# Ten input loads of a transformer block go to ScalarE's DMA queue, the others ahead of the row copies on SyncE's

## The chip, the cores and the metric

One NeuronCore of a Trainium2 chip runs the whole program. The metric is the device time of one execution in microseconds (us); the compared value is the median of several runs. A separate execution was taken with the hardware profiler; all tables and views come from that one.

## What is computed

A float32 block over x of 8 x 512 x 256: layer norm, 16-head attention, layer norm, residual, then a feed-forward layer with a top-1 choice among 8 low-rank experts, layer norm, residual. Cut to what matters:

```python
x_proj = (x @ w_in.T + b_in).reshape(b, l, h, -1)      # after layernorm of x
q, k, v = jnp.split(x_proj, 3, axis=-1)
att = softmax(jnp.einsum('blhd,bmhd->blmh', q, k) * scale, axis=2)
opt = jnp.einsum('blmh,blhd->blhd', att, v).reshape(b, l, d)
x = x + _layernorm(opt @ w_out.T + b_out)
...
top1 = argmax(softmax(x @ gate_W.T + gate_b))
base = x @ wi_W.T + wi_b
for i in range(8):
    inter = relu(base + (x @ lora_A[i].T) @ lora_B[i].T)
    out = out + (top1 == i) * (inter @ wo_W.T + wo_b)
x = x + _layernorm(out)
```

In the einsum for opt the key index m appears in att alone, so att is summed over it. The kernel forms all scores, their row maxima, exponentials and sums, as the reference does.

## The kernel before

The eight sequences are worked on one after another; a sequence has 512 tokens, in four chunks of 128 rows, and its 16 heads are taken in eight pairs. Every float32 operand of a matmul is split into a high and a low part (names that end in h and l), and a product is made of three matmuls. TensorE's projections (`psqk`, `psv`), the scores (`sc`), the output projection (`psy`) and the feed-forward layer (`psh`, `psz`) all run this way, the scores with the split laid out in rows by DMA.

The work is recorded as operations with an engine, a cost and a due time; a planner (`Plan.order`) plays them through and writes one list, and `settle` then moves some of them by hand. The program is emitted in the order of that list, so each engine gets its own part of the list in that order, and executes it strictly in order.

The head of the program, in the order in which its steps depend on each other:

- `load_x` (line 263) loads a sequence into `xt_b`; the first comes in two halves of 256 KB, the others in one piece of 512 KB. `load` (line 276) loads a weight; `fetch` (line 314) cuts a large weight into loads of 256 KB: `wv`, `wout`, and `wi_0` to `wi_3`, `wo_0` to `wo_3`. All of them are issued by SyncE.
- `first_weights` (line 1098): ScalarE scales `wqk_0` and makes its high part `wqkh`, VectorE its low part `wqkl`; then the same for `wqk_1`. These are ScalarE's first operations.
- `prepare` (line 496) for sequence 0: VectorE's statistics `st_x`, `mv_x` and the normalized `ln_x`; transposes `pst_xn` on TensorE; ScalarE's high part `xnh`, VectorE's low part `xnl`. On VectorE `wqkl` of `wqk_0` stands ahead of `ln_x`.
- `project` (line 536): six matmuls for each of four `psqk` tiles; ScalarE's and VectorE's parts go to `hl`.
- `lay_out_q` and `lay_out_k` (lines 579 and 559): SyncE copies `hl` to `q` and `rows`, two copies for each pair of heads, so that a score product has high and low parts in one pass.
- `scores` (line 618): the product `sc` on TensorE, the maximum `nmax` on VectorE, the exponential on ScalarE.
- `gate_weights` (line 1144): VectorE's `lbh` and `lbs` from `lb`; `wga` from `wga_f`. GpSimd splits `wv`, `wout`, `wi` and `wo`; before them it has the small operation `calm` (line 1250), which reads `ln_x`.

`warm_up` (line 1064) issues 30 matmuls on constants at the start.

In the built program every DMA signals one of eight completion semaphores, which are given out in turn. A DMA is issued only when the one that used its semaphore before has landed; the issuing engine waits for it, and so does what stands behind it on that engine. Before the change SyncE's order is: xt_0 (two), wqk_0, wqk_1, bqk, wv, wout, lb, wi_0 to wi_3, xt_1, xt_2, xt_3, wga_f, gb, low, bv, bout, wob, q_0 (two), rows_0 (two), q_1, rows_1, wo_0 to wo_3, q_2, rows_2, rows_3 and so on. The ninth, wi_0, is the first with a wait of this kind, for xt_0's first half; wga_f waits for lb, q_0 for xt_2 and xt_3.

In the part of `settle` at the change, `behind(last, ops)` takes `ops` out of the list and puts them in right after `last`; `of(engine, names...)` finds operations by the tile they write; `turns` are VectorE's first three operations that write `hl` of sequence 0.

Of the kernel before, what the change touches and what calls it, by code (L numbers as in the profile page):

```python
# [26 lines left out]
PE, ACT, DVE, POOL, DMA = "PE", "ACT", "DVE", "POOL", "DMA"  # L27
# [155 lines left out]
def kernel(  # L183
# [18 lines left out]
    nc = tc.nc  # L202
# [45 lines left out]
    def const_tile(shape, dtype, name, parts=1):  # L248
        return plan.tile(const, shape, dtype, name, 1, name)
# [6 lines left out]
    behind = [0.0]  # L256

    def landing(size):

        behind[0] = max(0.0, behind[0] + size / DMA_RATE - DMA_COST)  # L260
        return DMA_DELAY + size / DMA_RATE + behind[0]

    def load_x(b):
        t = xts[b] = plan.tile(io, [P, NC, D], F32, "xt", XB, f"xt_{b}")
        m = X0 if b == 0 else NC
        for c in range(0, NC, m):
            plan.op(
                DMA, DMA_COST,
                lambda c=c: nc.sync.dma_start(
                    out=t()[:, c : c + m],  # L270
                    in_=x[b].rearrange("(p c) d -> p c d", c=NC)[:, c : c + m],
                ),
                writes=[t], lag=landing(m * P * D * 4),
            )

    def load(name, src, shape=None, rows=P, place=None):

        shape = shape or list(src.shape)
        if place is None:
            t = const_tile(shape, F32, name)  # L280
        else:
            t = plan.tile(place[0], shape, F32, *place[1:], name)
        plan.op(
            DMA, DMA_COST, lambda: nc.sync.dma_start(out=t()[:rows], in_=src), writes=[t],
            lag=landing(rows * np.prod(src.shape[1:]) * 4),
        )
        return t

    def on_all_partitions(name, src):
        return load(name, src.partition_broadcast(P), [P, src.shape[0]])  # L290
# [23 lines left out]
    def fetch(name, src, *places):  # L314

        fs = flat(src).rearrange("p (c d) -> p c d", d=D)
        return [
            load(f"{name}_{i}", fs[:, 2 * i : 2 * i + 2], [P, 2, D], place=places[i % len(places)])
            for i in range(fs.shape[1] // 2)
        ]  # L320
# [23 lines left out]
    for i in range(2):  # L344
        t = const_tile([P, 2 * P], F32R, f"axs{i}")
# [146 lines left out]
    def units(b):  # L492

        return (0, 1), (2, 3)
# [590 lines left out]
    def fetch_first():  # L1085
        parts = [
            load(f"wqk_{dc}", wqk[:, dc], [P, 2, NG, P], place=(work, "full", FB))
            for dc in range(ND)
        ]
        return load("bqk", bqk), parts  # L1090

    during(-9000, "first", load_x, 0)
    wqk_in = during(-8990, "first", fetch_first)
    during(5000, "warm", warm_up)
# [36 lines left out]
    for g in range(NG):  # L1131
        during(-7000 if g == 0 else 0, f"project0{g}", project, 0, g)
        for p in range(NP * g, NP * (g + 1)):
            during(-6000 + 2 * p, "k0", lay_out_k, 0, p)
    during(0, "x1", load_x, 1)
    wv_h, wv_l = during(0, "wv", weight, "wv", wv.shape, wv_in, (POOL, POOL))

# [46 lines left out]
    for b in range(B):  # L1184
        t = 2 * STEPS * b
        if b + 2 < B:
            behind[0] = 0.0
            during(t, "load", load_x, b + 2)

        apart = units(b) if b in APART else [(0, 1, 2, 3)]  # L1190
        for i, cs in enumerate(apart):
            for p in range(NPR):
                at = t + STEPS * i + p * len(cs)
                during(at if b or i else at - 6000, "q" if b or i else "q0", lay_out_q, b, p, cs)
                scores(b, cs, p, at)
        if b + 1 < B:
            during(t, "prepare", prepare, b + 1)
            for g in range(NG):
                during(t, f"project{g}", project, b + 1, g)
                for p in range(NP * g, NP * (g + 1)):  # L1200
                    n = 2 if b + 1 in APART else 4
                    during(t + n * p, "k", lay_out_k, b + 1, p)
        for u in range(len(units(b))):
            tu = t + STEPS * (u if b in APART else 1)
            left = 2 * B - 1 - (2 * b + u)
            k = f"_{left}" if left < 3 else f"_first{u}" if b == 0 else f"{u}"
            during(tu, "v" + (k if b == 0 else ""), values, b, u)
            during(tu, "attend" + k, attend, b, u)
            during(tu, "feed" + k, feed, b, u)

    def settle(done):


        def of(eng, *marks):
            return [o for mark in marks for o in done if o.eng == eng and o.mark == mark]

        def behind(last, ops):
            for o in ops:
                done.remove(o)
            i = done.index(last) + 1  # L1220
            done[i:i] = ops


        behind(of(DVE, "ln_x_0_2")[-1], of(DVE, "bqk"))
        lbh = of(DVE, "lbh_0", "lbh_512")
        behind(of(DVE, "xnl_0")[-1], lbh)
        st2, turns = of(DVE, "st_x_2"), of(DVE, "hl_0_0_0", "hl_0_0_1", "hl_0_1_0")
        st1, maxes = of(DVE, "st_x_1"), of(DVE, "nmax_0_0_1_1", "nmax_0_2_0_1")
        behind(turns[0], st1[:2])
        behind(turns[1], st1[2:] + of(DVE, "mv_x_1"))  # L1230
        behind(turns[2], st2[:2])
        behind(maxes[0], st2[2:] + of(DVE, "mv_x_2"))
        behind(of(DVE, "nmax_0_2_0_1")[0], of(DVE, "st_x_3", "mv_x_3"))
        lbs = of(DVE, "lbs")
        behind(of(DVE, "nmax_0_1_1_1")[0], lbs[:1])
        behind(of(DVE, "nmax_0_3_0_1")[0], lbs[1:])
        behind(of(DVE, "nmax_0_4_1_1")[0], of(DVE, "wga"))


        nr = [[o for o in done if o.eng == POOL and o.mark == f"nr_x_{i}"] for i in range(4)]  # L1240
        wih, wil = of(POOL, "wih"), of(POOL, "wil")
        woh, wol = of(POOL, "woh"), of(POOL, "wol")
        behind(of(DVE, "mv_x_1")[-1], nr[1] + [wih[2], wil[2], wih[3], wil[3]])
        behind(of(DVE, "mv_x_2")[-1], nr[2])
        behind(of(POOL, "ln_x_2_2")[-1], nr[3])
        behind(
            [o for o in of(POOL, "ln_x_3_0")][-1], [woh[0], wol[0], woh[1], wol[1]]
        )
        behind(of(POOL, "hl_1_0_0")[-1], [woh[2], wol[2], woh[3], wol[3]])
        calm = Op()  # L1250
        calm.eng, calm.mark = POOL, None
        calm.fn = lambda: nc.gpsimd.tensor_scalar(
            calm_sb(), state[0]["xn"]()[:, 1, :1], 1.0, 0.0, ALU.mult, ALU.add
        )
        last = of(DVE, "ln_x_0_2")[-1]
        early = [o for o in done[done.index(nr[0][-1]) + 1 : done.index(last)] if o.eng == POOL]
        behind(last, early)
        done.insert(done.index(last) + 1, calm)


        rows = []
        for p in range(NP):
            if p < X1B:
                rows += of(DMA, f"q_0_{p}")
            rows += of(DMA, f"rows_0_{p}")
            if p == 1:
                rows += of(DMA, "wo_0", "wo_1", "wo_2", "wo_3")
        behind(turns[1], rows)


        extra = of(PE, "psu")[FIRST:]
        return [o for o in done if o not in extra]

    done = settle(plan.order())

    name = f"{B - 1}_{units(B - 1)[-1][0]}"
# [70 lines left out]
DMA_COST = 440.0  # L1347
# [20 lines left out]
XB = 4  # L1368
# [72 lines left out]
```

## Time and profile before

| | |
|---|---|
| median of 3 runs | 516.54 us (516.49 to 519.35) |
| profiled execution, time | 513.44 us |
| profiled execution, span from the first to the last instruction | 511.6 us |
| mean granted TensorE clock | 0.963 of full speed |
| busy: TensorE / VectorE / ScalarE / GpSimd | 95% / 91% / 85% / 76% of the span |
| chain that ended last | PE 62%, DVE 24%, ACT 4%, DMA 3% |
| loads, KB and us from issue to landing | xt_0 halves 256 KB 2.7; wqk 256 KB 4.4 and 4.6; wv 4.3; wout 4.7; wi 256 KB 6.4; wo 256 KB 4.5 (median); xt_1 to xt_3 512 KB 7.8 (median); rows 128 KB 2.9 (median) |

PE is TensorE, DVE VectorE, ACT ScalarE, POOL GpSimd, SP SyncE; SPq is SyncE's work of issuing DMAs. Times are counted from the span's start. The span lies 1.8 us under the time of its own execution, and that time 3.1 us under the median of the timed runs. The table shows averages; the head of the program has its own limits, which have to be read from the timeline and the chain of waits there.

### The profile page before, as it was taken

The page shows a single profiled execution, that of the slowest core. Times are in us where ns is not written, and L with a number is a line of the kernel's source. Part 1 is how long each engine was busy: PE and PEld are TensorE (multiplying, and loading weights), DVE is VectorE, ACT ScalarE, POOL GpSimd, SP SyncE. Part 2 cuts the span into 40 slices and gives each one's busy share as a digit, 9 for nine tenths or more (in the row PEclk, how much of TensorE's full clock was granted, in tenths as well). Part 3 has the DMA queues.
Part 4 walks back from the last instruction along what each step waited for, and adds up shares of the span by engine and source line. Part 5 has one row for each costly group of instructions (what it writes and reads, how often), then busy time and mean ns, then how long its engine had stood idle before and what let it go on. Part 6 is the DMA issues. An engine that isn't in the chain of part 4 may idle for free.

```text
span 511.6 us, 11203 instructions
## 1 busy us (share of the span) xinstructions
PE 483.8 (95%) x3134; PEld 423.7 (83%) x3134; DVE 467.3 (91%) x1056; ACT 436.4 (85%) x1205; POOL 390.1 (76%) x615
## 2 busy tenths in 40 slices
PE   7769989999999999999999999999999999998995
PEld 6534837879888988989989988989899988998995
DVE  6788999999999999999999999999999999998633
ACT  3569999998999999998999899999999989995210
POOL 7867455565889987997979998696878767888652
PEclk9955879999999999999999999999999999999999
DMA  8772263334423443244423442244224432200001
GB/s 273 217 196 68 52 154 71 89 69 112 111 51 106 113 111 68 69 121 104 105 50 120 101 102 75 51 113 110 66 70 94 114 87 67 48 26 2 21 22 42
DMA packets 41182, 46.56 MB, mean 91 GB/s; under 512 B 11326, under 2 KB 28222, under 8 KB 41120
## 3 DMA queue, kind: packets, MB, share of 16 engines
q1 hardware_dynamic: 41120, 45.84, 35.2%
q8 instruction: 26, 0.43, 0.3%
q14 instruction: 36, 0.29, 0.2%
HBM read 8.05 MB, written 4.19 MB: 24 GB/s over the span
## 4 chain that ended last, share of the span: by engine, by line
PE 62%; DVE 24%; ACT 4%; DMA 3%; issue 2%; SPq 2%; POOL 1%; POOLq 0%; ACTq 0%; DVEq 0%
PE sc L642 16%; PE psz L486 14%; DVE nmax L661 13%; PE psh L486 12%; PE psqk L486 7%; PE psy L486 3%; ACT sc L670 3%; PE psv L486 3%; PE psh L960 2%; DVE st_x L399 2%; PE sc L651 1%; DMA q<-hl 1%; DMA rows<-hl 1%; DVE hTh L300 1%; PE pst_x L469 1%
## 5 line engine op out<-in xcount | busy, mean ns | idle before, releaser
L670 ACT ACTIVATE sc<-sc,nmax 128x512 f32<-128x512 f32 x512 | 342.6, 689 | 17.1 <-DVE nmax L661 10.6
L661 DVE TENSOR_REDUCE nmax<-sc 128x1 f32<-128x512 f32 x512 | 325.4, 678 | 9.2 <-PE sc L651 4.2
L642 PE MATMUL sc<-rows,q 128*128 128x512 f32 x480 | 182.6, 423 | 5.6 <-ACT sc L670 3.1
L670 ACT ACTIVATION_READ_ACCUMULATOR sc<-sc,nmax 128x1 f32 x512 | 120.6, 236 | 0.0
L642 PEld LDWEIGHTS sc<-rows,q 128*128 128x128 f32 x480 | 88.7, 192 | 25.7 <-ACT sc L670 18.7
L486 PE MATMUL psz<-woh,hTh 128*128 128x256 f32 x256 | 73.0, 285 | 0.8 <-DVE xnl L528 0.5
L486 PE MATMUL psh<-x2h,wih 128*128 128x256 f32 x256 | 73.0, 285 | 0.0
L486 PE MATMUL psz<-woh,hTl 128*128 128x256 f32 x256 | 72.2, 282 | 0.0
L486 PE MATMUL psz<-wol,hTh 128*128 128x256 f32 x256 | 72.1, 282 | 0.0
L486 PE MATMUL psh<-x2h,wil 128*128 128x256 f32 x256 | 72.0, 281 | 0.0
L486 PE MATMUL psh<-x2l,wih 128*128 128x256 f32 x256 | 72.0, 281 | 0.0
L306 POOL TENSOR_TENSOR hTl<-full_h,hTh 128x512 fp32r<-128x512 f32 x44 | 56.9, 1294 | 2.3 <-DVE hTh L300 1.1
L486 PEld LDWEIGHTS psz<-wol,hTh 128*128 128x128 f32 x256 | 48.2, 188 | 3.6
L486 PEld LDWEIGHTS psh<-x2l,wih 128*128 128x128 f32 x256 | 48.2, 188 | 3.2
L486 PEld LDWEIGHTS psz<-woh,hTh 128*128 128x128 f32 x256 | 48.2, 188 | 2.1 <-POOL hTl L306 0.7
L486 PEld LDWEIGHTS psh<-x2h,wih 128*128 128x128 f32 x256 | 48.3, 189 | 1.1 <-DVE y L777 0.2
L486 PEld LDWEIGHTS psz<-woh,hTl 128*128 128x128 f32 x256 | 48.2, 188 | 0.2 <-POOL hTl L306 0.2
L486 PEld LDWEIGHTS psh<-x2h,wil 128*128 128x128 f32 x256 | 48.2, 188 | 0.0
L306 POOL TENSOR_TENSOR hl<-full_qk,hl 128x512 fp32r<-128x512 f32 x28 | 36.3, 1295 | 1.2
L384 ACT ACTIVATE full_h<-psh 128x512 f32<-128x512 f32 x44 | 26.4, 605 | 8.6 <-PE psh L960 8.1
L298 POOL TENSOR_SCALAR hl<-full_qk 128x512 fp32r<-128x512 f32 x28 | 17.3, 619 | 18.2 <-ACT full_qk L384 17.5
L486 PE MATMUL psqk<-xnh,wqkh 128*128 128x512 f32 x64 | 27.6, 431 | 0.7 <-ACT xnh L521 0.7
(132 smaller groups left out, 1021.4 us busy)
## 6 DMA issues: line engine op xcount, KB each, us to landing
rows<-hl SPq DMA_DIRECT2D x128, 128.0 KB, 2.6
q<-hl SPq DMA_DIRECT2D x480, 32.0 KB, 2.0
out<-ln_z SPq DMA_DIRECT2D x15, 256.0 KB, 2.2
xt<-in_x SPq DMA_DIRECT2D x7, 512.0 KB, 3.8
wi<-in_wi SPq DMA_DIRECT2D x4, 256.0 KB, 6.4
q<-hl SPq DMA_DIRECT2D x16, 64.0 KB, 2.2
wo<-in_wo SPq DMA_DIRECT2D x4, 256.0 KB, 4.5
xt<-in_x SPq DMA_DIRECT2D x2, 256.0 KB, 2.7
```

The costliest lines, as they stand in the source:

```text
L298: nc.gpsimd.tensor_scalar(pick_hi(), pick(), 1.0, 0.0, ALU.mult, ALU.add)
L300: nc.vector.tensor_copy(pick_hi(), pick())
L306: e.tensor_tensor(pick_lo(), pick(), f32(pick_hi()), ALU.subtract)
L384: lambda: nc.scalar.activation(full(), flat(ps()), func, **kw()),
L399: DVE, 335, lambda c=c: nc.vector.bn_stats(st()[:, c, :], sel()[:, c, :]),
L469: nc.tensor.transpose(ps()[:, dc, c * P : (c + 1) * P], src()[:, c, dc * P : (dc + 1) * P], ident(),)
L486: nc.tensor.matmul(ps, w, xx, start=start and i == 0, stop=stop and i == len(terms) - 1)
L642: nc.tensor.matmul(sc(), q()[:, e, cols], k(), start=True, stop=True)
L651: nc.tensor.matmul(sc(), q()[rows, 0, cols], k()[rows], start=True, stop=True)
L661: lambda sc=sc, nmax=nmax: nc.vector.tensor_reduce(nmax(), sc(), AX.X, ALU.max, negate=True),
L670: lambda sc=sc, nmax=nmax, esum=esum, i=i, h=h: nc.scalar.activation(sc(), sc(), AF.Exp, bias=nmax(), accum_out=esum()[:, i, h : h + 1]),
L960: nc.tensor.matmul(ps()[:, i, :], lbs()[:KL, fs], axs()[:KL, : n * P], start=False, stop=i == 1,)
```

## The change

```diff
@@ load_x
-                lambda c=c: nc.sync.dma_start(
+                lambda c=c: (nc.scalar if 0 < b < XB else nc.sync).dma_start(
@@ load
+        queue = nc.scalar if name.split("_")[0] in ("wv", "wout", "lb", "wi") else nc.sync
...
-            DMA, DMA_COST, lambda: nc.sync.dma_start(out=t()[:rows], in_=src), writes=[t],
+            DMA, DMA_COST, lambda: queue.dma_start(out=t()[:rows], in_=src), writes=[t],
@@ settle
+        behind(
+            of(DMA, "bqk")[-1],
+            of(
+                DMA, "wv_0", "wout_0", "lb", "xt_1", "wi_0", "wi_1", "wi_2", "wi_3", "xt_2", "xt_3",
+                "bv", "low", "wo_0", "wo_1", "wo_2", "wo_3", "wga_f", "gb", "bout", "wob",
+            ),
+        )
+
         rows = []
         for p in range(NP):
             if p < X1B:
                 rows += of(DMA, f"q_0_{p}")
             rows += of(DMA, f"rows_0_{p}")
-            if p == 1:
-                rows += of(DMA, "wo_0", "wo_1", "wo_2", "wo_3")
         behind(turns[1], rows)
```

XB is 4, so xt_1, xt_2 and xt_3 go to ScalarE's queue. The orders of TensorE, VectorE and GpSimd are those of before; ScalarE's differs by the ten loads, and SyncE's by the loads. The built program has them in these orders, with the load whose landing each one waits for in brackets:

- ScalarE: wv, wout, lb, xt_1, wi_0 [xt_0, second half], wi_1 [lb], wi_2 [wqk_0], wi_3 [xt_1], xt_2 [bv], xt_3 [wi_1]; then the load of the activation table, and the first operation on wqk_0.
- SyncE: xt_0 (two), wqk_0, wqk_1, bqk [wv], bv [xt_0, first half], low [wout], wo_0 [wqk_1], wo_1 [bqk], wo_2 [low], wo_3 [wi_0], wga_f [wi_2], gb [wo_0], bout [wi_3], wob [wo_1], q_0 [xt_2; wo_2], rows_0 [wo_3; xt_3], q_1, rows_1, q_2, rows_2, rows_3 and so on.

## The prediction

> **What bounds the kernel now.** I read the shares of the chain of waits first, for what sets the end, and then only the head in order of time, because the change touches nothing behind the first 25 us. TensorE is on 62% of that chain and VectorE on 24%; no transfer is waited for in the steady part. So whatever the head loses or wins is handed on whole to the end, unless a stage behind it has slack. The chain in order of time (start, length, what), cut to the head:
>
> ```profile
> 1.64 4.38 DMA wqk<-in_wqk
> ...
> 6.04 0.43 ACT wqk L1106
> ...
> 6.49 0.64 ACT wqkh L302
> ...
> 7.77 1.38 DVE ln_x L452 x4
> ...
> 11.02 2.97 DVE lbh L1166 x2
> ...
> 25.60 3.82 DMA rows<-hl
> ...
> 30.36 1.28 DVE nmax L661 x2
> ```
>
> The head is a string of short steps that begins when ScalarE gets wqk at 6.04. VectorE's ln_x stands in VectorE's order behind wqkl_0, which waits for ScalarE's wqkh_0; the transposes wait for ln_x, the projections for the transposes. From 18 to 25.6 the chain runs along SyncE, which issues rows one after another; then VectorE's maxima take over. Second, the timeline of the issuing engine and of ScalarE's first instruction (start, length, engine, line, what):
>
> ```profile
> 0.72 1.28 ACT L1106 ACT_TABLE_LOAD   x1 [0.72 <-PEq L1425]
> 0.73 0.87 SPq L269 DMA_DIRECT2D xt<-in_x  x2
> 4.52 2.56 SPq L284 DMA_DIRECT2D wi<-in_wi  x4
> 7.13 2.02 SPq L269 DMA_DIRECT2D xt<-in_x  x3
> 10.71 0.33 SPq L284 DMA_DIRECT2D wga_f<-in_wga  x1
> 21.67 2.01 SPq L284 DMA_DIRECT2D wo<-in_wo  x4
> ```
>
> ScalarE's table load is free today: it lies in the 5.3 us before wqk lands. SyncE is through with xt_3 at 9.15 and then stands until 10.71. Third, the queue's own waits up to 40 us (who waited for what: total, times, longest):
>
> ```profile
> SPq L593 <- DMA xt<-in_x: 1.6, 2, 0.9
> SPq L284 <- DMA lb<-in_lb: 1.5, 1, 1.5
> ```
>
> That is the fact on which all turns: a load waits for the landing of the load that last used its completion semaphore, and everything queued behind it on the issuing engine waits too. wga_f stood 1.5 us for lb; q_0 stood for xt_2 and xt_3. Fourth, the head cut into stretches of TensorE's clock window (TensorE, its weight load, VectorE, ScalarE, GpSimd busy; granted clock; DMA):
>
> ```profile
> 17.06:20.48 3.42, 2.73 (x18) 2.14 (x16) 1.14 (x3) 0.65 (x2) 3.17 (x6) 1.00 0.49 118
> 20.48:23.89 3.41, 0.74 (x4) 0.30 (x4) 3.00 (x5) 3.01 (x10) 2.67 (x3) 0.88 0.67 166
> 23.89:27.30 3.41, 1.38 (x4) 0.79 (x4) 3.41 (x11) 2.89 (x9) 2.06 (x5) 0.50 0.90 301
> ```
>
> One window with 0.74 us of work, and the clock is halved.
>
> **The ten loads on ScalarE.** They stand in front of everything ScalarE computes, the table load included, and six of them wait: wi_0 for xt_0's second half, wi_1 for lb, wi_2 for wqk_0, wi_3 for xt_1, xt_2 for bv, xt_3 for wi_1. Issuing alone: wv 0.43, wout 0.43, lb 0.47, five and more at the same lengths (wi 4 x 0.43 at most, xt 3 x 0.64), some 0.05 between: 5.4 us, so ScalarE could be free at 6.1 and, after the table load of 1.28, at 7.4. That is 1.4 later than now and the floor.
>
> The waits ask for more. The chain is lb lands, wi_1 is issued, wi_1 lands, xt_3 is issued. I count kilobytes. Now, lb lands at 10.7 as the last of 1930 KB (xt_0 512, wqk 512, bqk 2, wv 256, wout 256, lb 392); wout, at 1538 KB, lands at 8.2 (issue 3.53 plus 4.7). The four wi land 0.67 apart (the issues at 11.13, 11.82, 12.49 and 13.16 each follow a wait), so the full stream is 256 KB in 0.67, or 382 KB/us. With two queues feeding the same DMA engines I assume equal shares: when ScalarE's first 904 KB (wv, wout, lb) are through, so are 904 KB of SyncE's, 1808 in all. Slow end: on the old curve between wout and lb, 8.2 + 270/392 x 2.5 = 9.9. Fast end: full stream from the start, 0.73 + 2.0 (the shortest 256 KB load takes 2.7, of which 0.67 is stream) + 1808/382 = 7.5. From there wi_1 has 1024 KB in its own queue up to its end (xt_1, wi_0, itself), and SyncE's queue adds the last 120 of wqk and up to 768 of wo_0 to wo_2: 1144 to 1912 KB, 3.0 to 5.0 us. So wi_1 lands at 10.5 to 14.9. Then xt_3's issue 0.64, the table load 1.28, gaps 0.1: ScalarE touches wqk at 12.5 to 16.9 instead of 6.04, a delay of 6.5 to 10.9. I take the middle, 8.7, as nothing in the trace shows two queues side by side. (wi_3's wait for xt_1 and xt_2's for bv end before wi_1 lands: xt_1 is ahead of wi_1 in the same queue, bv right behind wqk_1.)
>
> The Trainium skill ("DMA: Bandwidth & Descriptors", section "Issuing engines are not separate DMA queues") speaks against the change: loads issued from several engines run on the same 16 DMA engines and interleave, and only the issuing time is saved. This trace has one queue alone, with DMA busy at 0.99 in 6.83 to 10.24, so no run here shows it yet; were it wrong, the stream above could be faster than 382 KB/us, and the delay would go towards the floor.
>
> Queued behind the delay: on ScalarE wqk, wqkh and all of hl; on VectorE wqkl_0 and so ln_x, the bias, xnl, lbh; on TensorE the transposes; on GpSimd "calm" and the weight splits behind it. None of it has slack against wqk today: ln_x starts 1.73 after wqk and will again. So 8.7 reaches hl whole. xt_0 and wqk themselves land later by sharing, but before ScalarE is free, hence at nothing; if that cover went, they would cost what ScalarE's wait now costs.
>
> **The loads that stay on SyncE, and wo ahead of rows.** bqk, bv, low, wga_f, gb, bout and wob are needed after 9 us plus delay; they cost nothing. The four wo leave the row issues: 2.05 us (21.67 to 23.72) that stood between rows_1 and q_2. Also gone are q_0's waits for xt_2 and xt_3: with hl 8.7 later, both have landed. q_0 can then go at 14.7 (hl_0_0_0 done) and ten issues later, from rows_0 at 16.0 and 0.63 each, rows_2 is out at 22.3, not 25.6; with the median landing of 2.9 in place of 3.82 it is there at 25.2, not 29.4. (These times are old ones, to be read plus the delay.) But 4.2 us are not won: what is late next is VectorE. After hl_0_1_1 ends at 21.3 it has four maxima 2.48, half a st_x and mv 1.09, four maxima 2.45, lbs 0.88, in sum 6.9, so the maxima of rows_2 start at 28.2 instead of 30.36. Gain: 2.1.
>
> **TensorE's clock.** The warm-up matmuls end at 7.4; the transposes now begin at 8.23 plus 8.7 = 16.9. At least two windows are empty, so by the fourth view the clock is halved. Three psqk matmuls took 1.58 at half clock and 0.70 at full. The 48 projections from 10.44 to 19.8 then run slow until a busy window has passed: none to 3.4 us lost (half of 6.8, two windows). I take 1.5, since the transposes themselves already load the array. It goes to hl_0_1_1 and from there to the maxima: the gain of 2.1 shrinks to 0.6; bounds a gain of 2.1 and a loss of 1.3.
>
> The Trainium skill ("TensorE: Matmul & The Clock Gate", section "What's actually happening") has a free-running window of 3413 ns and the full clock back after one busy window; by that rule the loss would be 1.7, half a window, and the sum 0.2 higher. No row here shows the clock come back after so long an idle stretch.
>
> **Sum.** +8.7 - 0.6 = +8.1; ends 6.5 - 2.1 = +4.4 and 10.9 + 1.3 = +12.2. On the profiled execution (513.4, span 511.6): 521.5. The three timed runs have a median of 516.5, 3.1 above it, with the same program; the difference carries over: 524.6.
>
> **Rivals.** (1) ScalarE is released early, and the time is not slower. Two queues together would have to stream much faster than 382 KB/us, so that every wait is over when its load comes up; then the delay is the floor of 1.4, the warm clock holds, and 1.4 - 2.1 = -0.7: 515.8. It decides where the delay falls below 2.1, that is where wi_1 lands by about 6.1. Against it: wi_1's wait is behind lb, third in its queue, and no load of 256 KB took under 2.7. I give all from -0.7 to +4.4 0.14. (2) The queues do not share equally: ScalarE's large loads hold back SyncE's, or lb keeps a 6.7 us flight (4.01 to 10.7) and wi_1 its 6.4 to 6.6 after it. Then wi_1 lands at about 1.9 + 6.7 + 6.5 = 15.1 or, with rates split unevenly, some 3 us later, and the clock costs its 1.3: +12.2 to +16, up to 532.5. 0.10. (3) The low-clock stage from 23 to 53 shrinks because its rows come sooner. From 40.96 to 51.20 VectorE is busy 8.46 of 10.24, so 1.8 is there at most; with (1) that makes -2.5, not 1%. 0.02 for anything faster than 1%.
>
> **Chances.** The forecast, +4.4 to +12.2, has 0.74. One per cent, 5.2 us, is about what a measurement can tell from no change. Of the forecast some 0.06 lies below 5.2. So slower: 0.74 - 0.06 + 0.10 = 0.78; within 1%: 0.14 + 0.06 = 0.20; faster 0.02, which I round up to 0.04 and take from within. Range: 519.5 to 530, from +3 to +13.5, which leaves out (1)'s lower part and (2)'s upper.
>
> **What would show it.** ScalarE's first rows are ten issues, with idle time before wi_1 that ends with lb, and before xt_3 that ends with wi_1; the table load behind them at 11 to 15; wqk at 12.5 to 16.9. SyncE has no wait for xt between q_0 and rows_2. The clock reads 0.50 where the transposes begin. From the maxima of rows_2 on, all is old time plus a constant. I am wrong if wqk is touched before 9, if the table load stays at 0.72, or if the head's delay is caught up behind 30 us.

## The result, and the profile after

The changed kernel takes 525.28 us (median of 4 runs, 522.33 to 526.02) against 517.2 us before (median of 4, 516.49 to 519.35): a ratio of 1.0139, with a 95% interval of 1.0109 to 1.0170. Its profiled execution took 522.33 us with a span of 520.5 and a mean granted clock of 0.952; that of before had 513.44, 511.6 and 0.963. The two spans differ by 8.9, the two medians by 8.1.

First, ScalarE's timeline after the change, from the start to its first operation on wqk (start, length, engine, line, operation; ACTq is ScalarE's work of issuing DMAs):

```profile
0.72 0.41 ACTq L285 DMA_DIRECT2D wv<-in_wv  x1
1.17 0.45 ACTq L285 DMA_DIRECT2D wout<-in_wout  x1
1.65 0.69 ACTq L285 DMA_DIRECT2D lb<-in_lb  x1
2.36 0.36 ACTq L269 DMA_DIRECT2D xt<-in_x  x1
5.60 5.29 ACTq L285 DMA_DIRECT2D wi<-in_wi  x4
11.24 1.61 ACTq L269 DMA_DIRECT2D xt<-in_x  x2
12.88 1.28 ACT L1107 ACT_TABLE_LOAD   x1 [12.88 <-DMA wi<-in_wi]
14.18 0.42 ACT L1107 ACTIVATE wqk<-wqk 128x256 f32<-128x256 f32 x1
```

Four loads go out by 2.7. Then the queue stands until 5.60 (wi_0 waits for the second half of xt_0), and a row of four wi that takes 5.29 holds more waits: taken apart, wi_1 is issued at 8.56, wi_2 at 8.94, wi_3 at 10.56, then xt_2 at 11.24 and xt_3 at 12.52. The table load comes last and wqk is touched at 14.18, 8.14 later than before. The table load's bracket says what ended the wait. The first of ScalarE's waits in the first 25 us (who waited for what: total, times, longest), and in the same form some of SyncE's when issuing, up to 60 us:

```profile
ACT L1107 <- DMA wi<-in_wi: 12.9, 1, 12.9
```

```profile
SPq L594 <- DVE st_x L400: 5.9, 1, 5.9
SPq L285 <- DMA wqk<-in_wqk: 4.0, 1, 4.0
SPq L285 <- DMA wo<-in_wo: 3.7, 2, 2.2
...
SPq L594 <- DMA xt<-in_x: 0.3, 1, 0.3
```

All of ScalarE's first 12.9 us is one wait in this view, put down to wi_1's landing. SyncE now waits longer for loads than before, but these waits end by 18.6; the last of them, 0.3, is q_0's for xt_2. Only then comes the longest: q_0, issued at 23.89, waits 5.9 us for compute. Before the change the two copies of q_0 waited 1.6 us in all for xt. (st_x is what the profile sees last; q_0 needs hl.)

The chain of waits in order of time (start, length, what):

```profile
16.36 2.09 PE pst_xn L470 x8
19.12 6.64 PE psqk L487 x18
25.76 2.88 PE psv L487 x24
28.64 1.42 PE psqk L487 x6
...
31.55 2.39 DVE nmax L662 x4
33.94 0.66 DVE st_x L400 x2
34.60 0.28 DVE mv_x L405 x4
34.88 2.37 DVE nmax L662 x4
37.25 0.80 DVE lbs L1172
38.05 1.20 DVE nmax L662 x2
```

Between the projections and the maxima of rows_2 the chain of before ran along SyncE's issues of rows, up to a landing of 3.82. Now no SPq row stands there: from 31.55 VectorE works without a gap until 38.05. Last, the head in stretches of TensorE's clock window (TensorE, its weight load, VectorE, ScalarE, GpSimd busy; granted clock; DMA share; GB/s):

```profile
6.83:10.24 3.41, 0.81 (x7) 0.61 (x6) 0.00 (x0) 0.00 (x0) 1.21 (x2) 0.96 1.02 329
10.24:13.65 3.41, 0.00 (x0) 0.00 (x0) 0.00 (x0) 0.77 (x1) 0.00 (x0) 0.50 0.91 227
13.65:17.06 3.41, 0.70 (x3) 0.56 (x4) 1.77 (x5) 2.50 (x5) 0.00 (x0) 0.50 1.02 350
17.06:20.48 3.42, 2.73 (x10) 1.79 (x9) 2.95 (x6) 1.20 (x2) 3.12 (x5) 0.50 0.97 359
20.48:23.89 3.41, 3.41 (x10) 2.69 (x9) 2.40 (x4) 0.69 (x1) 3.33 (x3) 0.54 0.05 16
23.89:27.30 3.41, 3.41 (x24) 3.05 (x23) 2.82 (x10) 1.38 (x2) 2.26 (x5) 1.00 0.20 46
```

In 10.24 to 13.65 no engine computes, apart from ScalarE's table load. The clock is at half from 9.9 to 23.6: 10 matmuls fill the fifth stretch, and 24 the sixth.

How the delay travels, as start in the profiled execution after minus before (the orders of TensorE and VectorE are the same, so rows can be paired one by one):

| | before | after | shift |
|---|---|---|---|
| ScalarE touches wqk | 6.04 | 14.18 | 8.14 |
| last of the 24 psqk | 19.40 | 29.64 | 10.24 |
| first maxima | 21.65 | 31.47 | 9.82 |
| maxima of rows_2 | 30.35 | 37.97 | 7.62 |
| VectorE's maxima up to 160 us | | | 7.6 |
| the same at 350 us, then the last of them | | | 7.9, 8.87 |

### The profile page after: what moved, and what is told of

Read it like the earlier page. It is cut to its first block, busy times and chain, and to the rows that moved or that the text cites. A ratio compares the mean times of both kernels' runs of the same rounds, so it can differ in the third digit from the quotient of the medians.

```text
span 520.5 us, 11201 instructions
## 1 busy us (share of the span) xinstructions
PE 489.2 (94%) x3134; PEld 426.5 (82%) x3134; DVE 467.4 (90%) x1056; ACT 437.1 (84%) x1205; POOL 390.1 (75%) x615
## 4 chain that ended last, share of the span: by engine, by line
PE 67%; DVE 22%; DMA 5%; ACT 2%; issue 2%; POOL 1%; SPq 1%; POOLq 0%; ACTq 0%; DVEq 0%
PE sc L643 16%; PE psz L487 14%; DVE nmax L662 14%; PE psh L487 12%; PE psqk L487 8%; PE psv L487 3%; PE psy L487 3%; PE psh L961 2%; DMA q<-hl 2%; DMA wqk<-in_wqk 2%; DVE st_x L400 1%; PE sc L652 1%; ACT sc L671 1%; PE pst_xn L470 1%; PE psg L812 1%
## 5 line engine op out<-in xcount | busy, mean ns | idle before, releaser
L643 PEld LDWEIGHTS sc<-rows,q 128*128 128x128 f32 x480 | 88.8, 191 | 26.9 <-ACT sc L671 18.5
```

Source lines behind the costliest of these rows:

```text
L643: nc.tensor.matmul(sc(), q()[:, e, cols], k(), start=True, stop=True)
```

## Experiments

The theory to be tested: ScalarE stands behind loads that wait for other loads to land, and this wait, with half a clock window or so and minus what the rows win, is the whole difference. The rivals: the new order on SyncE costs the time; the second queue slows the early loads; issuing, not waiting, holds ScalarE; the clock alone costs it.

Each kernel was timed against the kernel before on the same chip. All shifts below are against the profiled execution of before, in us; "delay" is the shift of ScalarE's first touch of wqk, the last but one column the difference of the medians.

| kernel | delay | last psqk | first maxima | maxima of rows_2 | medians | ratio (95%) |
|---|---|---|---|---|---|---|
| after | 8.14 | 10.24 | 9.82 | 7.62 | +8.1 | 1.0139 (1.0109 to 1.0170) |
| e1_sync_only | -0.67 | -0.66 | 3.06 | 0.88 | -0.8 | 0.9981 (0.9962 to 1.0001) |
| e3_four_on_scalar | 2.48 | 4.02 | 3.59 | 1.39 | +0.8 | 1.0026 (0.9993 to 1.0058) |
| e6_eight_on_scalar | 6.14 | 8.17 | 7.75 | 5.55 | +5.2 | 1.0099 (1.0067 to 1.0131) |
| e4_warm | 8.58 | 11.88 | 13.25 | 11.07 | +13.7 | 1.0233 (1.0168 to 1.0299) |
| e4b_warm_front | 8.30 | 9.24 | 8.82 | 6.62 | +6.1 | 1.0118 (1.0075 to 1.0161) |
| e10_table_early | 7.04 | 9.85 | 9.43 | 7.23 | +7.2 | 1.0141 (1.0102 to 1.0179) |
| e2_wo_back | 8.03 | 9.87 | 9.45 | 7.97 | +8.3 | 1.0152 (1.0118 to 1.0186) |
| e7_wo_later | -0.46 | 0.10 | 0.17 | -1.94 | -0.4 | 0.9983 (0.9953 to 1.0014) |
| e8_wo_scalar_idle | -0.16 | 1.06 | 3.83 | 1.64 | +0.9 | 1.0005 (0.9976 to 1.0033) |

In seven of the ten the shift at the maxima of rows_2 and the difference of the medians agree within 0.8; e1's and e7's differ by 1.7 and 1.5, e4's by 2.6. So the head decides the time, about one to one. One caution: e1, e7 and e8 begin with the same loads as before, up to lb, and still touch wqk 0.16 to 0.67 earlier. Differences of half a microsecond between two profiled executions can be chance.

**e1_sync_only.** All loads on SyncE, in the new order; wo stays out of the rows.

```diff
-                lambda c=c: (nc.scalar if 0 < b < XB else nc.sync).dma_start(
+                lambda c=c: nc.sync.dma_start(
...
-        queue = nc.scalar if name.split("_")[0] in ("wv", "wout", "lb", "wi") else nc.sync
+        queue = nc.sync
```

> The changed kernel with all loads on SyncE again; their new order, with wo ahead of the row copies, is kept. Theory (ScalarE's loads hold back its first operation on wqk): wqk is touched at about 6.0 again, not 14.2; rows_0 waits until the last wo has landed, about 20, 2 us later than before the change, and the maxima of rows_2 start at about 31 (30.4 before, 38.0 in the changed kernel); time 0 to 2 us over before. Rival (loads and wo ahead of the rows are what costs): the maxima of rows_2 stay near 38 and the time 6 us or more over before.

The ratio is 0.9981 (0.9962 to 1.0001): the order alone costs nothing that can be measured. ScalarE touches wqk at 5.37 and the last psqk is 0.66 early. The first maxima are 3.06 late all the same: rows_0 is issued at 20.58, behind wo and the small loads, which wait for one another up to 18.6. By rows_2 0.88 of it is left. So the order is ruled out as the cause; the queue is what counts.

**e3_four_on_scalar.** Only the four loads that wait for nothing (wv, wout, lb, xt_1) stay on ScalarE.

```diff
-                lambda c=c: (nc.scalar if 0 < b < XB else nc.sync).dma_start(
+                lambda c=c: (nc.scalar if b == 1 else nc.sync).dma_start(
...
-        queue = nc.scalar if name.split("_")[0] in ("wv", "wout", "lb", "wi") else nc.sync
+        queue = nc.scalar if name.split("_")[0] in ("wv", "wout", "lb") else nc.sync
```

> Only the first four loads stay on ScalarE's queue (wv, wout, lb, xt_1), none of which waits for a semaphore; the other six go back to SyncE in the same order, wo still ahead of the rows. Theory: ScalarE's queue is free at 2.7, the table load ends near 4, and wqk_0 is touched when it lands, at about 8.3 as in the changed kernel (shared stream), wqk_1 near 10.4; the delay is 2 to 3 us instead of 8.1, the clock stays full for the projections, and the time is 0 to 2 us over before. Rival (two queues at once slow the loads, and that is the 8 us): the delay stays over 6 us and the time 6 us or more over before.

ScalarE's timeline in this kernel, behind its four issues:

```profile
2.74 1.28 ACT L1107 ACT_TABLE_LOAD   x1 [2.74 <-issue]
8.52 0.42 ACT L1107 ACTIVATE wqk<-wqk 128x256 f32<-128x256 f32 x1 [4.49 <-DMA wqk<-in_wqk]
```

Without loads that wait, ScalarE is free at 4.02, and the delay falls from 8.14 to 2.48. The time goes back with it, to 1.0026 (0.9993 to 1.0058). The 2.48 that remain go with the second queue: wqk lands at about 8.5, beside wv, wout and lb, and in e1, where the same loads stand behind it in one queue, ScalarE touches it at 5.37. After the change the same late landing (8.3) is hidden behind ScalarE's wait, as the prediction said. What I expected of the clock was wrong: TensorE's gap is only 7.6 to 10.7, and still the clock is at half from 9.9 to 16.7; of the 4.02 at the last psqk 1.54 are the clock's.

**e6_eight_on_scalar.** xt_2 and xt_3 go back to SyncE; the four wi stay.

```diff
-                lambda c=c: (nc.scalar if 0 < b < XB else nc.sync).dma_start(
+                lambda c=c: (nc.scalar if b == 1 else nc.sync).dma_start(
```

> xt_2 and xt_3 go back to SyncE, at their places in the order; ScalarE keeps eight loads, the last of which, wi_3, waits for xt_1. Theory (the chain of semaphore waits sets ScalarE's start): the waits for bv and for wi_1 leave ScalarE, it is through at about 10.9, the table load ends near 12.2 and wqk is touched at about 12.3: delay 6.2 instead of 8.1, time about 2 us under the changed kernel. Rival (the number of issues, not the waits, sets it): two issues of 0.33 less, delay 7.5, time within 1 us of the changed kernel.

```profile
6.03 4.83 ACTq L285 DMA_DIRECT2D wi<-in_wi  x4
10.89 1.28 ACT L1107 ACT_TABLE_LOAD   x1 [10.89 <-DMA xt<-in_x]
12.18 0.42 ACT L1107 ACTIVATE wqk<-wqk 128x256 f32<-128x256 f32 x1
```

Two issues fewer, some 0.7 of work, win 2.00 of delay; the timeline shows why. The last wait is now wi_3's, for xt_1, and it ends before 10.9; after the change xt_3's wait for wi_1 ended only at 12.5. The medians differ from before's by 5.2 instead of 8.1, so waits hold ScalarE, not issuing.

**e4_warm and e4b_warm_front.** 100 warm-up matmuls on constants instead of 30, to keep the clock up through the gap; all else is that of the changed kernel. The planner records 100, and `settle` leaves out those past `FIRST`. e4_warm only raises that number:

```diff
-FIRST = 30
+FIRST = 100
```

e4b_warm_front puts the other 70 right behind the first 30 instead of leaving them out:

```diff
-        extra = of(PE, "psu")[FIRST:]
+        warm = of(PE, "psu")
+        behind(warm[FIRST - 1], warm[FIRST:])
+        extra = []
```

> The changed kernel with 100 warm-up matmuls instead of 30, so that TensorE works until about 15.7, just before the transposes at 16.4. Theory: wqk is still touched near 14.2 (delay 8.1), the clock reads 1.00 where the projections begin, the first maxima come 7.6 to 8.1 after those of before instead of 9.8, the maxima of rows_2 about 5.5 after instead of 7.6, and the time is about 2 us under the changed kernel. Rival (the clock cost nothing, because something else paces the first maxima, such as the rows): the shifts stay at 9.8 and 7.6 and the time does not move.

> The changed kernel with all 100 warm-up matmuls in one row ahead of the transposes (e4's extra ones were spread among the projections by the planner's order, so that it did not test the clock). Theory (the idle stretch of TensorE costs about 2 us by the halved clock): the warm-up ends near 15.8, the clock reads 1.00 under the transposes and projections, wqk is touched near 14.2 as in the changed kernel, the first maxima come 7.7 to 8.2 after those of before instead of 9.8, the maxima of rows_2 5.4 to 6.0 after instead of 7.6, time about 2 us under the changed kernel. Rival (the clock hides behind the rows or VectorE): shifts of 9.8 and 7.6 stay.

e4_warm missed its aim, as one row of its TensorE timeline shows:

```profile
18.95 4.26 PE L1072 MATMUL psu<-ones 128*128 128x256 f32 x20
```

The planner put most of the added matmuls between the transposes and the projections and behind them, where they are on the path: 13.7 us more than before, which tells nothing of the clock. e4b_warm_front does test it. Its stretches in the view of the windows (columns as above):

```profile
11.70:15.10 3.40, 3.40 (x31) 3.40 (x29) 0.00 (x0) 2.01 (x3) 0.00 (x0) 1.00 0.88 260
15.10:18.50 3.40, 1.72 (x10) 0.90 (x8) 3.04 (x8) 2.28 (x5) 0.97 (x2) 1.00 1.02 392
18.50:21.90 3.40, 3.17 (x7) 2.27 (x8) 3.40 (x4) 0.18 (x1) 3.40 (x4) 0.50 0.63 217
```

The clock is full up to 18.5, with ScalarE as late as after the change (8.30). The difference between delay and first maxima falls from 1.68 to 0.52. It doesn't vanish: between 15.1 and 18.5 the end of the warm-up and the transposes fill TensorE for 1.72 of 3.40, and the clock is halved for the window after. So the halved clock costs the changed kernel about 1.2 us at the first maxima; in the time this can't be told from the changed kernel (1.0118, interval 1.0075 to 1.0161).

**e10_table_early.** A copy of 128 x 1 elements on ScalarE right behind xt_1 pulls the table load forward, into the first wait.

```diff
+    tbl_sb = const_tile([P, 1], F32, "tbl")
...
+        early = Op()
+        early.eng, early.mark = ACT, None
+        early.fn = lambda: nc.scalar.activation(
+            tbl_sb(), mhalf()[:, :1], AF.Copy
+        )
+        done.insert(done.index(of(DMA, "xt_1")[0]) + 1, early)
```

> The changed kernel with one more operation on ScalarE, a copy of a 128x1 constant behind its fourth load, so that the table load runs while ScalarE waits for xt_0; all waits between loads are as they were. Theory (the delay is the end of the last wait plus xt_3's issue plus the table load): table load at 2.8 to 4.1, wqk touched at about 12.9 instead of 14.2, maxima of rows_2 about 6.3 after those of before instead of 7.6, time 1.3 us under the changed kernel. Rival (wqk's own landing or VectorE sets the start): wqk is touched near 14.2, no change.

```profile
2.74 1.28 ACT L1273 ACT_TABLE_LOAD   x1 [2.74 <-issue]
...
13.08 0.42 ACT L1108 ACTIVATE wqk<-wqk 128x256 f32<-128x256 f32 x1 [8.84 <-DMA wi<-in_wi]
```

The load of 1.28 is out of the path and wqk is touched 1.10 earlier. In the time nothing of it shows (1.0141, interval 1.0102 to 1.0179; the interval is too wide to exclude the 1.3 that was expected), and the trace has the last psqk only 0.39 earlier. In this execution the clock came back at 24.1, in that of after at 23.6, so the projections that begin earlier run longer at half speed. As an estimate, 1.10 us more at half speed are worth 0.55, and the edge that lies 0.5 later takes 0.25 back, which leaves 0.3. An earlier start inside a slow window is worth half of itself at most, and where the edge lies decides the rest; that is read from one execution of each kernel.

**e2_wo_back.** The change, but the four wo stand between rows_1 and q_2 again.

```diff
-                "bv", "low", "wo_0", "wo_1", "wo_2", "wo_3", "wga_f", "gb", "bout", "wob",
+                "bv", "low", "wga_f", "gb", "bout", "wob",
...
+            if p == 1:
+                rows += of(DMA, "wo_0", "wo_1", "wo_2", "wo_3")
```

> The changed kernel with the four wo back between rows_1 and q_2. The semaphores are then given out otherwise: xt_3 waits for wi_0, which waits for lb, so ScalarE's delay should be 7 to 8.2. Theory (with the halved clock VectorE's maxima come late anyway, and the 2.05 us that wo took on SyncE are mostly unused): maxima of rows_2 0 to 1 us later against the delay than in the changed kernel, time within 1 us of the changed kernel. Rival (taking wo out of the rows is worth its 2 us in full): time 2 us over the changed kernel at the same delay.

The chain of waits of this kernel near rows_2:

```profile
29.32 0.58 SPq L285
...
32.63 0.61 SPq L573
...
33.28 4.10 DMA rows<-hl
...
37.52 0.81 PE sc L652 x2
38.33 1.28 DVE nmax L662 x2
```

With wo back, the chain runs along SyncE again and ends in a landing of rows, as before the change. Between the first maxima and those of rows_2 the kernel wins 1.48 instead of 2.20. So taking wo out is worth 0.7 here. The other 1.5 must come from the change's other effects on the rows; that q_0 no longer waits for xt, and that rows are issued while VectorE still has its first maxima to do, is likely and was not separated. Nor is 0.7 a fixed price: in the kernel before, moving wo alone is worth 2.1 between the same two points (e7, below).

**e7_wo_later and e8_wo_scalar_idle.** Both start from the kernel before and move only wo: behind rows_2, or to ScalarE's queue behind hl_0_1_0.

```diff
-            if p == 1:
+            if p == 2:
```

```diff
+        queue = nc.scalar if name.split("_")[0] == "wo" else nc.sync
...
-            DMA, DMA_COST, lambda: nc.sync.dma_start(out=t()[:rows], in_=src), writes=[t],
+            DMA, DMA_COST, lambda: queue.dma_start(out=t()[:rows], in_=src), writes=[t],
...
-            if p == 1:
-                rows += of(DMA, "wo_0", "wo_1", "wo_2", "wo_3")
         behind(turns[1], rows)
+        behind(of(ACT, "hl_0_1_0")[-1], of(DMA, "wo_0", "wo_1", "wo_2", "wo_3"))
```

> The kernel before, all loads on SyncE in their old order, with the four wo moved from behind rows_1 to behind rows_2. Theory (in the kernel before, rows_2 is what the maxima wait for, 2.1 us at most): the maxima of rows_2 start about 2 us earlier, near 28.2; if nothing behind them is late in turn the time is up to 2 us under before. Rival (rows_3, now behind wo, is late instead, or a later stage takes the gain back): the maxima of rows_3 stand where they were and the time is that of before.

> The kernel before, with the four wo alone on ScalarE's queue, behind its third operation on hl, where ScalarE stood idle for 3.8 us (16.06 to 19.83); everything else stays on SyncE in the old order. Theory (what a load on ScalarE costs depends on where its wait lies): ScalarE issues the four in about 1.5 us of idle time, wqk is touched near 6.0, hl_0_1_1 is not late, the rows lose 2.05 us of SyncE, and the maxima of rows_2 start 1.5 to 2.1 us before those of the kernel before; at the end 0 to 2 us under before. Rival (a later stage, at half clock, takes the gain back as in the run with wo behind rows_2): earlier at rows_2, not at the end.

e7 wins 1.94 at the maxima of rows_2, yet the time does not move (0.9983, interval 0.9953 to 1.0014): the shift is -0.98 at VectorE's 13th maxima, -0.63 at the 24th and +0.33 at the 50th. The first half of the gain goes where the rival put it, to what now stands behind wo: in e7's chain of waits a copy to q, issued at 30.23, lands at 32.94, and the scores ahead of the 13th maxima wait for it. For the rest, the stage at half clock ends at 54.5 in e7 and at 53.8 in before; whether the edge of the window took it or something else is not separated.

e8 did not do what I expected. Rows of its timeline:

```profile
18.43 2.51 ACTq L285 DMA_DIRECT2D wo<-in_wo  x4
18.93 1.19 SPq L573 DMA_DIRECT2D rows<-hl  x2
20.46 0.39 PE L487 MATMUL psqk<-xnh,wqkl 128*128 128x512 f32 x1
20.98 0.69 ACT L363 ACTIVATE hl<-psqk,bqk 128x512 fp32r<-128x512 f32 x1 [5.10 <-DMA wo<-in_wo]
24.93 0.33 PEld L652 LDWEIGHTS sc<-rows,q 64*128 64x128 f32 x4 [4.51 <-DMA rows<-hl]
25.47 2.48 DVE L662 TENSOR_REDUCE nmax<-sc 128x1 f32<-128x512 f32 x4 [3.02 <-PE sc L652]
```

I had taken ScalarE's idle time as free room. But wo_0 waited for wga_f, whose semaphore it takes; wga_f landed at 18.4, behind xt_3, and ScalarE was through with the four issues only at 20.94. The bracket of 5.10 looks like the mechanism of the change once more, but here the wait cost next to nothing. hl_0_1_1 needs the last psqk, and that is itself 1.06 late, because in this execution xt_1 landed at 15.6 instead of 14.4 and VectorE and TensorE waited in turn; hl_0_1_1 starts 0.52 after it, in before 0.43. What is late is rows_0. It is issued at 18.93, 1.08 later than before, and its two copies take 5.0 and 5.3 us to land, where 2.6 was measured before for the second. They land beside the loads of wo; that these hold them back is likely, but rests on one execution. The first maxima come 3.83 later by it. rows_1, now waiting for wo_0 to land, goes out at 22.53 instead of 20.39. No version that was run beats the kernel before beyond its interval.

## Why the prediction was right, step by step

**ScalarE's delay, +8.7: measured 8.14.** The mechanism was the one predicted, link by link. lb landed at 8.5 (7.5 to 9.9 was given) and released wi_1 at 8.56; wi_1 landed at 12.5 (10.5 to 14.9; the middle is 12.7), and xt_3 was issued at 12.52. e3 and e6 show that it is the cause: delay and time fall together as the waits are taken away, and e6 shows the chain's last link by itself. xt_3 was issued in 0.33 instead of 0.64. One detail differed: xt_2's wait for bv ended only at 11.2, not well ahead of wi_1, as SyncE issued bv at 5.07 and it took 6.1 to land. It still lay inside xt_3's wait and cost nothing.

That the middle of the range was met so closely is partly luck. From 8.56 to 12.52 the DMA moved 1.20 MB (1170 KB), 1.08 MB of it for ScalarE's queue and 0.12 for SyncE's, at 304 GB/s, or 297 KB/us. The sum had 1144 to 1912 KB at 382 KB/us. The bytes lay at its lower end, because SyncE stood for wqk_1 until 10.36 and had brought next to nothing of wo; at 382 they would have landed in 3.1 us. The stream was slower than assumed, and the two misses cancel: 3.96 us against a middle of 4.0.

**The transfers.** The sum assumed that two queues bring no more than 382 KB/us and share evenly. DMA in four stretches of 3 us after the change, then the last of the four before it:

```profile
1.50:4.50 3.00, 2.82 (x13) 2.82 (x14) 0.12 (x1) 0.00 (x0) 2.70 (x13) 1.00 0.76 248
4.50:7.50 3.00, 3.00 (x19) 2.94 (x18) 1.78 (x8) 0.00 (x0) 1.61 (x6) 1.00 1.06 354
7.50:10.50 3.00, 0.14 (x2) 0.00 (x0) 0.00 (x0) 0.00 (x0) 0.63 (x1) 0.91 1.01 328
10.50:13.50 3.00, 0.00 (x0) 0.00 (x0) 0.00 (x0) 0.62 (x1) 0.00 (x0) 0.50 0.89 219
```

```profile
10.50:13.50 3.00, 2.78 (x11) 2.08 (x12) 3.00 (x3) 0.69 (x1) 3.00 (x3) 1.00 1.05 404
```

In the first three, 248, 354 and 328 GB/s, or 2.79 MB; before it was 248, 337 and 271, or 2.57 MB. So two queues brought 9% more there, at the same busy share of the DMA engines (2.83 in sum, both times) and with no higher peak. The fourth stretch turns it round: over all 12 us two queues brought 3.45 MB, 9% less than the 3.78 of one. What made that stretch slow is open. A second queue alone does not do it: e3, with four loads on ScalarE's, moved 3.95 MB in the same 12 us. The shares were nearly even up to lb's landing: by 8.56 ScalarE's queue had moved 1.15 MB and SyncE's 0.97. The Trainium skill's rule ("DMA: Bandwidth & Descriptors", "Issuing engines are not separate DMA queues"), which spoke against the change, agrees with these rows as far as they go: the second queue brought no higher peak and kept the DMA engines no busier. It adds that issuing from several engines saves only issuing time; here even this was lost, as SyncE stood 4.0 us for wqk and ScalarE was not free before 12.9. Rivals (1) and (2) fall with it: wi_1 did not land by 6.1, and the uneven sharing that would have made 15.1 did not come.

**Loads on SyncE, nothing.** e1 bears it out for the time: 0.9981. The 0.88 that e1 shows at the maxima of rows_2 do not show in its median.

**wo out of the rows, and q_0's waits: gain 2.1, limited by VectorE.** Measured 2.20 between the first maxima and those of rows_2, and the chain shows VectorE without a gap there, as worked out: four maxima, st_x and mv, four maxima, lbs, 6.50 in all where 6.9 had been added up. How much of it is wo's place depends on the rest: with wo back (e2) 1.48 of the 2.20 remain, and with wo alone moved (e7) 2.11 are won. The two causes do not add up, since VectorE's own work, which the prediction named as the limit, stands under both.

**The clock, +1.5.** Measured 2.10 at the last psqk and 1.68 at the first maxima, inside the range of 0 to 3.4; the reason held too, half speed from 9.9 to 23.6. The Trainium skill ("TensorE: Matmul & The Clock Gate", "What's actually happening") has a free-running window of 3413 ns and the full clock back after one busy window; the rows agree, since the half-speed stretch of 13.7 is four such windows and ends with the first one that is filled with work. The estimate worked out from it, 1.7, stood nearer than mine.

**Net.** Gain minus clock is 0.5 where 0.6 was predicted, and 8.14 - 0.5 = 7.6, the shift up to 160 us. Rival (3), the stage at half clock, did shrink, from 30.7 us (23.1 to 53.8) to 27.3 (33.8 to 61.1). It ended 7.4 later, so this gave back nothing of the head's delay worth naming. The remaining 1.3 of the profiled difference comes late: 0.3 by 350 us and two jumps of about 0.5 at 363 and between 411 and 437. What makes them was not tested.

**The level.** The sum of +8.1 was put on a median 3.1 above the profiled execution of before. This carried over, since after's median is 2.95 above its own profiled execution, but by luck: in the nine experiments the profiled execution lies between 0.3 under its kernel's median (e10) and 2.95 over it (e3). The predicted 524.6 lies 0.7 under 525.28, because before's median is itself 517.2 with the fourth run, not 516.5.

## What to carry to other kernels

A load is not free on the queue of a compute engine. Find out which completion it must wait for, and count everything that the engine computes behind it as waiting too. A load that waits for nothing (e3's four) costs its issue; one that waits holds the engine up to that landing, and this costs what the engine had to do meanwhile: 8.14 us here, next to nothing in e8. Give a second queue only loads that are issued before the semaphores come round. Do not count on more transfer from it in the head (9% less over 12 us here, 4% more in e3), and expect the load that is wanted first to land later: wqk at 8.3 after the change and at 8.5 in e3, where one queue had it at 6.0 before and at 5.3 in e1.

## What was not expected of the hardware

**One lost clock window, late in the run.** In e3's profiled execution the shift against before is 2.98 at 417.5 and 5.82 at 421.8, far from the change. Its stretches there:

```profile
418.00:422.90 4.90, 3.06 (x22) 2.60 (x21) 3.09 (x9) 3.75 (x12) 1.70 (x2) 1.00 0.26 64
422.90:426.30 3.40, 3.40 (x16) 3.10 (x15) 1.95 (x6) 1.94 (x5) 1.89 (x2) 0.50 0.22 49
426.30:431.00 4.70, 4.69 (x35) 4.24 (x34) 4.54 (x11) 2.63 (x8) 3.40 (x7) 1.00 0.21 47
```

TensorE stands for a while (3.06 busy of 4.90), then one window of 3.4 us is granted at 0.50. In all 2.8 us are lost: 1.5 while TensorE stands, ahead of the window, and 1.35 in it. The shift grows by 1.3 to 1.7 at the same place in e6, e7 and e10 too, though their clock stays full there. The same single window is in e4, e4b, e2 and e8 between 421 and 436, and all five have a second one between 493 and 508; e6, e7 and e10 have just one, between 491 and 502. The profiled executions of before, after and e1 have none. It may explain how single runs scatter: over 54 timed runs of before, 514.16 to 521.3 us, time and mean granted clock (0.952 to 0.966) have a correlation of -0.79. That is not shown for each run, as only one was profiled.

**Short gaps cost whole windows.** In e3 a gap of 3.1 us in TensorE's work (7.6 to 10.7) brought two windows at half clock, 9.9 to 16.7; in e4b 1.72 us of work in a window did not keep the clock up.
